# Plain pointwise products, products of the four-by-four convolution copied by pairs of banks, and the padded image as two tiles

## The chip, the cores and the metric

The kernel runs on one core of one Trainium2 chip. The metric is the device time of one execution in microseconds (us). TensorE is called PE in the profile, its weight loads PEld, VectorE DVE, ScalarE ACT, GpSimd POOL; SP issues most of the DMAs.

## The reference

Eight images of 512 channels and 32 x 32 points in fp32 go through two layers, each added to its input. Cut to what matters:

```python
# layer 0, on group-normed x: a bottleneck with attention, twice
t = cbs(x, cv1_w, ...)                 # 1x1 conv, norm, silu: 512 -> 512
ys = [t[:, :C], t[:, C:]]              # C = 256
for i in range(2):
    yi = ys[-1]
    z = cbs(yi, m_cv1_w[i], ..., pad=1)        # 3x3 conv, 256 -> 256
    z = bot_attention(z, ...)                  # qkv, 4 heads of 64, softmax over 1024
    ys.append(yi + silu(bn(conv1x1(z, m_cv2_w[i]))))
x = x + cbs(concatenate(ys), cv2_w, ...)       # 1x1 conv, 1024 -> 512
# layer 1, on group-normed x
h = prune(relu(bn(depthwise3x3(x))), 4.0)      # a channel whose maximum is below 4 becomes 0
h = prune(relu(bn(conv1x1(h, pw_w))), 1e-3)    # the pointwise convolution, 512 -> 512
x = x + h
```

## The kernel before

Images are done one after another, but an image's layer 1 is spread over the next image's layer 0. Every piece of work is a small function that is filed under a short name, and four strings, `FIRST`, `HEAD`, `TAIL` and `LAST`, say in which order the pieces are issued: image 0 runs `FIRST`, images 1 to 6 run `HEAD` and `TAIL`, image 7 `HEAD` and `LAST`. Each engine executes its own instructions in exactly that order (class `InOrder`), so a piece that has to wait holds back all that stands behind it on its engine. `p*3` means the next three pieces filed under `p`. All instructions recorded through these helpers show one line, L105, in the profile, so they are told apart by their tiles.

A three-by-three convolution (`conv3(l)`, l = 0 and 1) is done by a four-by-four transform. `dr` (DVE) combines rows of the padded image `yp[l]`, `d` combines columns into three operands that lie in `kr`, `vt` and `qy` (j = 0, 1, 2), `P` multiplies (PE), `Rc` copies the products out of PSUM (ACT), `R` and `B` (DVE) are the row and column sums of the way back, `E` ends them, and `Ez` (ACT) writes `z`. There are nine `P` for each convolution: for each j, part 0 makes four products of output half m = 0, part 1 two of each half, part 2 four of m = 1. Each `P` has 32 matmuls of 64 columns, pops one tile of 1 MB weights from the ring `wring` (five buffers, loaded from DRAM by SP) and asks for the next load. Before, the PSUM tile of two banks belongs to (j, m): half m of one j fills 768 of its 1024 columns, and it is copied in two steps (512 after the part of four, 256 after the part of two), 12 copies in a convolution. These tiles come from a pool of two, `big`, which the scores, the queries, keys and values also use.

After the convolution come `k`, `v`, `q` (products with `wqkv`, tiles `ps_qk` and `ps_v`), `ka`, `va`, `qa` (their copies by ACT), attention in 32 steps (`s` scores, `e` exponentials, `w` values, `p` sums on DVE, `n`, `nr`, `ns`, `sc` the normalization), then `m`, `ma`, `mr`: the 1x1 convolution `ps_m`, its activation, and the residual, which for l = 0 is written into `yp[1]`.

The pointwise convolution of layer 1 is done before, for images 0 to 6, by seven products in place of eight on quarters of the matrices (`by_quarters`, `one_pair`): `ot` makes four differences of the image `ht` on DVE (written into `pt`), `o` and `O` are two times seven products of two matmuls each, `ok` and `Ok` are copies by ACT, `ou` and `Ou` two times seven additions on DVE, and `oa`, `Oa` the closing activations. Its weights are combined during image 0 (`combine_more`) and kept in DRAM. The products write tiles of one bank, `acc`, of which there are three; attention's value sums, `ps_y` and `ps_m` use the same three. In `HEAD` the pieces `o` and `O` stand around the end of the first attention and in the second convolution. For image 7 the product is plain and in `LAST`.

`dp` loads the next image into `pt` (four DMAs on SP), `g` and the names behind it norm it. `t` are the eight depthwise taps per group of 128 channels on DVE (`ht<-xn,v_sb,ht`). `to_rows` adds the result of layer 0 to `xt` while it brings the points from an order by phase back into rows.

Of the kernel before, what the change touches and what calls it, by code (L numbers as in the profile page):

```python
# [15 lines left out]
P = 128  # L16
# [29 lines left out]
    g*4 gm gd g*2 gv gp gb ga*2 g*2 gm gd ta0 c gv gp fo gb ga*2 ta0 c ta0 ti0*2 fo ti0 ta2 c ca  # L46
    ti0*3 to0*2 ta2*2 c rl ca ti2*6 dr*3 to2*2 y ya dr*4 ta1*3 ti1*6 to1*2 rl dr*6 y ya y dr*3
    d*8 ya y ya d P Rc P*2 Rc*3 R*4 P*2 Rc R Rc R Rc B P Rc R*2 P Rc B P Rc*2 R*2 E B*2 Ez P Rc
    R*2 E Ez dw k*2 X ta0*2 k ka kp k ka kp ta0 ti0*2 v*2 va ti0*3 v ti0 v va ta1 q*3 qa ta1 q qa
    ta1 s e to0 ti1 s e p s e w to0 s p e w*2 s e p ti1*5 s e p*2 w s e to1 s e p w p w s e to1  # L50
    ta2 s e w*2 h p z s e p ta2*2 ti2*2 s e w s e w*2 ti2*4 s e w s to2*2 w*2 e s e p*2 rh s e w
    s e p*4 w h z s*2 w e*2 n s e w p s p*2 w*2 nr e nr*3 s e nc s e ns p w s e w*2 nc s e p*2 w
    h z s e s w s*2 p*2 e p e*2 p sc p w*2 sc w s e p w s e w p w*2 h z n nr*4 ns nc sc Q K m ma
    sc dp mr m*2 ma mr m ma dr mr ma mr dr*15 d*2 Q K nc d P*3 Rc*3 d*3 P*2 Rc R*2 d R*2 P Rc*3 d
    R d R Rc R*2 P Rc B*2 P Rc R*2 Rc P Rc B E Ez R*2 B E Ez dx cw X k*4 ka kp ka kp v*2 q v va v
    va cw*2 rk cw q qa q*2 qa s*2 e*2 p s e p w s e w s p cw*2 e s e w s e p rk p w s e p*2 s e w
    s e g*2 w*3 p h z s e w cw s e p*2 cw*2 rk s e w*2 s e w s p e rk s w p s w e p g*2 e p s w
    g*2 e s e w p h z p s w e g p w n nr s e nr p w g s e s p w nr e s e w s p w*2 nr p e s e w h
    ns p s e p nc*2 s e p w*2 s e p w s*2 e p w sc e p s e p w sc w*3 h z n nr*4 ns Q z Q sc*2
    nc*2 m*2 ma mr ma mr m ma m ma mr gm mr gd Q gv u A Q x i u A x i gp i*2 Q gb ga*4 Q im id Q  # L60
    iv A Q x ip i*2 ib b bm t*3 Q A t x i*2
# [3 lines left out]
    t c*2 t b bm im id ca c iv t dr*3 t*2 dr ip l dr*3 c t ca ib b lr dr*6 y dr*3 d*3 y*2 P Rc t  # L65
    d t ya R d*4 P*2 Rc*2 P R Rc R*2 Rc P Rc R*2 d t Rc ya P Rc P B P Rc*3 R*2 bm R ya B R B E P
    Rc R Ez R B b bm E Ez lp y ya k*4 ka kd ka X kd t*5 v t v va l v*2 va t lr t*2 q*2 t qa q*2
    qa s e t s e lp p t s w e s l s w e s p*2 w e*2 p w s e s p w t s w t e s p lr e*2 w*2 p h z
    s e w s t w s p*2 s e p e w*2 s e*2 w s t e p*3 s w s e w e t p*2 w lp t h z s*2 e w s e*2
    p*3 s e n w*2 s e s e w nr*3 s e nr t p*2 ns p l w*2 s e p lr lp w*2 h ot s e s w p ot s w*2  # L70
    s e p nc e p e w p s e ot s e w*2 p*2 z sc w*2 h z n nr nc o O ok Ok nr*3 ns o ou oa O*2 Ou
    sc*2 Oa m sc m*2 ma*2 m nc mr Ou ot mr ma mr dr ma o nc mr ou dr*3 O dr*5 o ou dr*7 d*3 Ou O
    o d*6 ou Ou*2 P*2 Rc*2 ou P R*2 Rc*2 R oa O P*3 o P Rc R*2 Rc*4 R B*2 R*2 Oa Ou B R P Rc*2 R
    ou oa B Oa dp P Rc o E Ez R*2 E Ez O k v*2 va X Ou ou oa k*2 ka kd k ka kd fr f fr f Oa fr*2
    f*2 dx v*2 va q*3 qa q qa s e s*2 e p e p w s e w s*2 e*2 p*3 w s*2 g e*2 w*4 s p e s e w p
    s*2 h g e g p z w s w p e*2 s*2 e w*2 g*2 s p e*2 g p*3 g s w*3 e p s e w h z s e s e p*2 w*2
    s p e p s n nr*3 w e p s nr g e p s w*4 e p s nc e s ns e nc w s h s p w*2 e p e s w s*2 e*2
    z sc p w p e p*2 w s sc e p w*3 h n nr*4 ns z
# [3 lines left out]
    Q*2 K r2 Q*2 sc*2 m K r0 m r2 m r1 nc*2 ma mr m ma*3 mr r0*2 mr r0 r1*2 Q gm Q*2 mr r1 u0 a0  # L82
    r2 u1 r2 gd Q u0*2 r3*2 gv r3 Q a1 x1 r3 gp gb ga x0 u0*2 a0 Q u0 x0 a0 i x0 i Q*2 i ga u0 ga
    a0 i im x0 Q id iv ip Q u1*2 ib u1 b u1 bm ga Q i Q t*2 u1 t a1*2 x1*2 u1 i a1 i x1 t i
# [3 lines left out]
    sc nc Q nc m ma m sc m*2 ma rg mr*2 ma*2 mr*2 Q*2 A x Q i*2 im id rg iv ip ib b bm t Q*2 t A  # L88
    x i*2 Q im t*2 Q id iv ip t ib t b t Q bm Q*2 t*2 A t l x i*2 im t lr lp id t iv ip ib t A b
    t*2 bm t Q o A x t l lr x i*2 lp o*3 im o t id t o*2 iv ip t o ib b bm o t*7 l lr lp t*5 l lr  # L90
    lp o*17 oa o oa fr f o oa o oa fr f o*3 oa*2 fr f oa*2 fr f
# [34 lines left out]
def fast_kernel(  # L126
# [54 lines left out]
    def load(dst, b):  # L181
# [14 lines left out]
    yp = [const_tile([P, 2, 4, 4, ROWS], f"yp{l}") for l in range(2)]  # L196
# [21 lines left out]
    ]  # L218

    PRODUCTS = ("a11", "a12", "s2", "s1", "s3", "a22", "s4")  # L220
    q_dram = [
        [dram.tile([P, 7, 2, P], F32, tag=f"q{i}_{p}", name=f"q{i}") for p in range(2)]
        for i in range(2)
# [28 lines left out]
    for t in yp:  # L252
        nc.gpsimd.memset(t, 0.0)
# [43 lines left out]
    def half_of(l, m, n):  # L297

        if l == 0:
            t = yp[0][:, m, :, 2 * n : 2 * n + 2, F // 4 :]  # L300
        else:
            t = yp[1][:, n].rearrange("p q (r k) x -> p q r k x", k=2)[:, :, :, m, F // 4 :]
        return t.rearrange("p q r x -> p r q x")
# [99 lines left out]
    def ring_sources():  # L403
        for b in range(B):
            for l in range(2):
                if b and l:
                    for p in range(2):
                        yield q_dram[1][p].rearrange("p q k o -> p (q k o)"), 1792
                for i in range(9):
                    yield u_dram[l][i].rearrange("p a b c d -> p (a b c d)"), 2048  # L410
                yield wqkv[:, l].rearrange("p k o -> p (k o)"), 1536
                if b == l == 0:
                    for m in range(2):
                        yield w2[:, :, m * P : (m + 1) * P], 1024
# [102 lines left out]
    plain = []  # L517

    def plain_pw():

        if not plain:
            plain.append(ring.pop(0).rearrange("p (k o) -> p k o", o=C))
        return plain[0]

    def by_quarters(rights, names, pairs):

        src, sums = rights
        b11, b12, b21, b22 = (
            (lambda i=i, n=n: src[:, 2 * i : 2 * i + 2, n * 512 : (n + 1) * 512])
            for i in range(2)
            for n in range(2)
        )
        t1, t2, t3, t4 = ((lambda t=t: t.rearrange("p (k n) -> p k n", k=2)) for t in sums)

        def less(o, x, y):
            nc.vector.tensor_tensor(o(), x(), y(), ALU.subtract)  # L540

        add(
            names[0],
            lambda: less(t1, b12, b11),
            lambda: less(t2, b22, t1),
            lambda: less(t3, b22, b12),
            lambda: less(t4, b21, t2),
        )
        right = dict(a11=b11, a12=b21, s2=t2, s1=t1, s3=t3, a22=t4, s4=b22)
        for kinds, finish in zip(names[1:], pairs):  # L550
            one_pair(right, kinds.split(), finish)

    def one_pair(right, kinds, finish):
        banks, kept, w = {}, [], []

        def product(name):
            if not w:
                w.append(ring.pop(0)[:, :1792].rearrange("p (q k o) -> p q k o", k=2, o=P))
            banks[name] = bank_tile("ps_q")
            for k in range(2):  # L560
                nc.tensor.matmul(
                    banks[name],
                    w[0][:, PRODUCTS.index(name), k, :],
                    right[name]()[:, k, :],
                    start=(k == 0),
                    stop=(k == 1),
                )
            if name == PRODUCTS[-1]:
                ring_load()

        def keep():
            t = work_tile("kept")
            kept.extend((t[:, :512], t[:, 512:]))
            nc.scalar.copy(kept[0], banks["a11"])

        def plus(o, x, name):
            nc.vector.tensor_tensor(banks[name] if o is None else kept[o], kept[x], banks[name], ALU.add)

        add(kinds[0], *[lambda name=name: product(name) for name in PRODUCTS])
        add(kinds[1], keep)  # L580
        add(
            kinds[2],
            lambda: plus(None, 0, "a12"),
            lambda: plus(0, 0, "s2"),
            lambda: plus(1, 0, "s1"),
            lambda: plus(0, 0, "s3"),
            lambda: plus(None, 1, "s3"),
            lambda: plus(None, 0, "a22"),
# [156 lines left out]
    def conv3(l):  # L745
# [17 lines left out]

        def by_rows(n, step):

            y = yp[l][:, n]
            if l == 0:
                o = [slots[:, slot[k], :, n] for k in range(6)]
                both = slots[:, :2, :, n]
# [1193 lines left out]
```

## Time and profile before

| | |
|---|---|
| median of 3 runs | 2728.95 us (2728.0 to 2729.35) |
| the profiled execution | 2721.36 us |
| its span, first to last instruction | 2719.6 us |
| mean granted TensorE clock | 0.986 |
| busy: PE, DVE, ACT, POOL | 2541.0, 2197.2, 1302.8, 133.2 us |
| one image to the next (second convolution to second convolution) | 327.7 to 328.6 us |
| in the image from 527.3 to 855.5 us: PE, DVE, ACT busy | 314.3, 269.1, 159.5 us |

A record of the profile is one hardware instruction; a full fp32 matmul of the program is two records. A row of a group has the engine, the operation, output and inputs, the shapes, the count, the busy time in us, the mean ns of one, then the idle time of the engine just before and what ended it. In a timeline the first column is the start, the second the length of the merged instructions, and a bracket holds the idle time before them and its releaser. Records of one engine may overlap, so the mean length of one matmul is longer than the distance between two.

### The profile page before, as it was taken

How to read it: one execution, taken by the hardware profiler on the slowest of the kernel's cores; microseconds unless marked ns; L12 is line 12 of the kernel's file. 1: busy time of each engine (PE TensorE's matmuls, PEld its weight loads, DVE VectorE, ACT ScalarE, POOL GpSimd, SP SyncE). 2: the span in 40 equal slices, each digit the busy share in tenths (PEclk: the TensorE clock that was granted, in tenths of full speed). 3: DMA queues.
4: the chain of work that ended last, by engine and by line, in shares of the span. 5: the costliest groups of instructions: out<-in, count | busy, mean ns of one | idle time of the engine just before them, and what ended most of it. 6: DMA issues, size and time to landing. Idle time of an engine off the chain costs nothing. (4 is left out here: it accounts for less than half of the span.)

```text
span 2719.6 us, 49469 instructions
## 1 busy us (share of the span) xinstructions
PE 2541.0 (93%) x20950; PEld 1242.5 (46%) x20950; DVE 2197.2 (81%) x3354; ACT 1302.8 (48%) x1748; POOL 133.2 (5%) x111
## 2 busy tenths in 40 slices
PE   4898999999999999989999899998999999999997
PEld 2535454443545445353453534535345453544433
DVE  7987778877988779887788877887788877988657
ACT  3453446354463544635356354554436444463534
POOL 1100001000010000000000000000000000010000
PEclk8999999999999999999999999999999999999999
DMA  8657223261413414153240621407024171322400
GB/s 286 222 177 266 87 107 106 78 221 45 157 49 126 169 59 159 29 197 102 70 161 19 225 75 62 164 16 283 17 82 143 32 268 32 124 87 92 154 16 33
DMA packets 97285, 325.97 MB, mean 120 GB/s; under 512 B 8224, under 2 KB 44832, under 8 KB 76704
## 3 DMA queue, kind: packets, MB, share of 16 engines
q1 hardware_dynamic: 89472, 304.64, 31.1%
q0 software_dynamic: 4032, 14.68, 3.0%
q10 hardware_dynamic: 3552, 3.41, 0.4%
q8 instruction: 166, 2.72, 0.4%
q14 instruction: 63, 0.52, 0.1%
HBM read 262.67 MB, written 43.25 MB: 112 GB/s over the span
## 5 line engine op out<-in xcount | busy, mean ns | idle before, releaser
L105 ACT ACTIVATE e<-ps_s 128x1024 f32<-128x1024 f32 x512 | 506.8, 1023 | 263.5 <-PE ps_s L105 214.0
L105 PE MATMUL ps_s<-qy,kr 64*64 64x512 f32 x4096 | 509.6, 592 | 8.1 <-ACT e L105 6.4
L105 PE MATMUL ps_av<-e,vt 64*64 64x512 f32 x4096 | 501.8, 590 | 0.0
L105 DVE TENSOR_TENSOR sum<-sum,e 128x1024 f32<-128x1024 f32 x384 | 470.2, 1224 | 37.3 <-ACT e L105 14.1
L105 DVE SCALAR_TENSOR_TENSOR ht<-xn,v_sb,ht 128x961 f32<-128x961 f32 (+1 forms) x256 | 317.9, 1247 | 8.6 <-ACT ht L105 5.0
L105 PEld LDWEIGHTS ps_s<-qy,kr 64*64 64x64 f32 x4096 | 160.1, 132 | 298.0 <-issue 186.6
L105 PEld LDWEIGHTS ps_av<-e,vt 64*64 64x64 f32 x4096 | 166.5, 133 | 276.2 <-issue 269.6
L105 PE MATMUL ps_qk<-z,wring 128*128 128x512 f32 x512 | 228.7, 595 | 11.6 <-ACT vt L105 7.7
L105 ACT COPY c<-ps_c 128x512 f32<-128x512 f32 x192 | 87.5, 482 | 303.5 <-PE ps_c L105 278.3
L105 DVE TENSOR_TENSOR sum<-e 128x1024 f32<-128x1024 f32 x64 | 78.0, 1219 | 127.6 <-ACT e L105 127.6
L105 PE MATMUL ps_c<-kr,wring 128*64 128x64 f32 x3072 | 116.4, 245 | 58.2 <-DVE kr L105 46.1
L105 PEld LDWEIGHTS ps_qk<-z,wring 128*128 128x128 f32 x512 | 95.7, 190 | 127.9 <-issue 104.3
L105 PEld LDWEIGHTS ps_c<-kr,wring 128*64 128x64 f32 x3072 | 110.9, 159 | 74.7 <-DVE kr L105 52.3
L105 PE MATMUL ps_y<-pt,w_sb 128*128 128x512 f32 x256 | 114.9, 602 | 11.2 <-ACT y L105 11.2
L105 PE MATMUL ps_c<-vt,wring 128*64 128x64 f32 x3072 | 102.3, 223 | 24.0 <-ACT c L105 8.9
L105 PE MATMUL ps_c<-qy,wring 128*64 128x64 f32 x3072 | 101.2, 223 | 23.1 <-ACT c L105 14.0
L105 DVE RECIPROCAL r<-ps_dn 128x128 f32<-128x128 f32 x128 | 109.5, 912 | 8.7 <-PE ps_dn L105 8.7
L105 PE MATMUL ps_cv<-pt,w_sb 128*128 128x512 f32 x256 | 116.0, 604 | 0.0
L105 PE MATMUL ps_v<-wring,z 128*128 128x256 f32 x512 | 114.6, 379 | 1.1 <-DVE kr L105 1.1
L105 PE MATMUL ps_m<-z,wm_sb 128*128 128x512 f32 x256 | 112.5, 592 | 0.0
L105 PEld LDWEIGHTS ps_c<-vt,wring 128*64 128x64 f32 x3072 | 95.0, 138 | 35.0 <-issue 13.6
L105 PEld LDWEIGHTS ps_c<-qy,wring 128*64 128x64 f32 x3072 | 94.8, 138 | 33.2 <-ACT c L105 17.4
(181 smaller groups left out, 3453.5 us busy)
## 6 DMA issues: line engine op xcount, KB each, us to landing
wring<-u SPq DMA_DIRECT2D x144, 1024.0 KB, 6.4
pt<-in_x SPq DMA_DIRECT2D x32, 512.0 KB, 7.3
rw<-r SPq DMA_DIRECT2D x64, 256.0 KB, 3.4
xt<-in_x SPq DMA_DIRECT2D x32, 512.0 KB, 6.2
out<-xt SPq DMA_DIRECT2D x32, 512.0 KB, 5.5
kr<-r POOLq DMA_DIRECT2D x28, 512.0 KB, 6.5
wring<-q SPq DMA_DIRECT2D x14, 896.0 KB, 7.0
u<-ucomp SPq DMA_DIRECT2D x48, 256.0 KB, 3.0
```

The source lines that it names most:

```text
L105: made = method(*args, **kwargs)
```

## The change

- The pointwise convolution of images 0 to 6 is multiplied plainly: eight pieces `o`, each four matmuls into one bank, and eight `oa`. `by_quarters`, `one_pair`, `combine_more` and their DRAM tiles are gone; the weights `wpw` come through the ring as one tile of 1 MB.
- A product of `conv3` writes one whole bank. Products 2n and 2n+1 share a tile of two banks, and one copy of 1024 columns empties it; the ninth has its own copy of 512. Five copies take the place of twelve.
- `yp[l]` is two tiles, one for each half of the channels (l = 0) or of the rows (l = 1).
- `to_rows` makes four additions over pairs of adjacent words in place of two over every fourth word.
- The four order strings are written anew.

```diff
-    yp = [const_tile([P, 2, 4, 4, ROWS], f"yp{l}") for l in range(2)]
+    yp = [[const_tile([P, 4, 4, ROWS], f"yp{l}_{n}") for n in range(2)] for l in range(2)]
...
                 if b and l:
-                    for p in range(2):
-                        yield q_dram[1][p].rearrange("p q k o -> p (q k o)"), 1792
+                    yield wpw.rearrange("p k o -> p (k o)"), 2048
...
-    def by_quarters(rights, names, pairs):
-    def one_pair(right, kinds, finish):
...
         if b < B - 1:
-            pairs = [lambda ps, low, n, p=p: close(2 * p + low, n, ps) for p in range(2)]
-
-            by_quarters((h_all, pt), ("ot", "o ok ou oa", "O Ok Ou Oa"), pairs)
+            def whole(m, n):
+                banks[m, n] = bank_tile("ps_pw")
+                part(m, n, range(KC))
+                if (m, n) == every[-1]:
+                    ring_load()
+
+            add("o", *[lambda e=e: whole(*e) for e in every])
+            add("oa", *[lambda m=m, n=n: close(m, n) for m, n in every])
...
         def products(j, part):
             u = ring.pop(0).rearrange("p (x i k o) -> p x i k o", x=4, i=2, k=2)
+            g = 3 * j + part
+            if g // 2 not in banks:
+                banks[g // 2] = big_tile("ps_c3")
+            ps = banks[g // 2][:, g % 2, :]
             for x in range(4):
-                m, row = UNITS[4 * part + x]
-                if (j, m) not in banks:
-                    banks[j, m] = big_tile("ps_c3")
-                ps = flat(banks[j, m])
+                row = UNITS[4 * part + x][1]
                 for i in range(2):
-                    at = place[row] * P + i * HD
+                    at = x * P + i * HD
...
-        def rows_copy(j, m, part):
-
-            if (j, m) not in copies:
-                copies[j, m] = work_tile("c1")
-            c = slice(0, 512) if part == 0 else slice(512, 768)
-            nc.scalar.copy(copies[j, m][:, c], flat(banks[j, m])[:, c])
+        def rows_copy(n):
+
+            t = copies[n] = work_tile("c1")
+            if n < 4:
+                nc.scalar.copy(t, flat(banks.pop(n)))
+            else:
+                nc.scalar.copy(t[:, :512], banks.pop(n)[:, 0, :])
...
-        for r in range(2):
-            nc.vector.tensor_tensor(o[..., r], i[..., r], o[..., r], ALU.add)
+        for q in range(4):
+            nc.vector.tensor_tensor(o[:, :, q], i[:, :, q], o[:, :, q], ALU.add)
...
-            combine_more(1, wpw)
```

Of the orders, the stretch of `HEAD` from the first `m` of the first attention to the second convolution's keys shows how they change:

```diff
-    sc*2 Oa m sc m*2 ma*2 m nc mr Ou ot mr ma mr dr ma o nc mr ou dr*3 O dr*5 o ou dr*7 d*3 Ou O
-    o d*6 ou Ou*2 P*2 Rc*2 ou P R*2 Rc*2 R oa O P*3 o P Rc R*2 Rc*4 R B*2 R*2 Oa Ou B R P Rc*2 R
-    ou oa B Oa dp P Rc o E Ez R*2 E Ez O k v*2 va X Ou ou oa k*2 ka kd k ka kd fr f fr f Oa fr*2
+    p z p sc w*2 h n nr*2 z nc nr*2 ns o*2 oa o oa sc*2 m sc m*2 ma*2 nc mr*2 dr*2 m dr*2 ma*2 mr
+    o oa dr*4 mr dr*6 o*2 oa dr*2 d*3 P*2 d nc d oa P d*4 P*2 Rc*2 P Rc R o P*3 o R*5 B*2 R oa R
+    B Rc B Rc R*2 E Ez R*2 E Ez k*4 fr f ka kd ka kd X q oa*2 q*3 dp qa*2 v fr f fr*2 f*2 dx v va
```

And the first convolution of `HEAD`, from its first `d` to the keys:

```diff
-    ... d*3 y*2 P Rc t d t ya R d*4 P*2 Rc*2 P R Rc R*2 Rc P Rc R*2 d t Rc ya P Rc P B P Rc*3 R*2
-    bm R ya B R B E P Rc R Ez R B b bm E Ez lp y ya k*4
+    ... d*2 y d y*2 t d t d*2 P*2 d P*2 Rc d R d ya Rc P*2 Rc P b P R*3 Rc R*2 ya R B R*2 B R B bm
+    E P Rc Ez R B R E Ez bm ya t*6 lp y k*3
```

## The prediction

> **What bounds the kernel now.** I read part 1 of the page first, then the table of waits of PE, then the timeline around one three-by-three convolution, then the groups kept apart by shape.
>
> ```profile
> PE 2541.0 (93%) x20950; PEld 1242.5 (46%) x20950; DVE 2197.2 (81%) x3354; ACT 1302.8 (48%) x1748; POOL 133.2 (5%) x111
> ```
>
> PE (TensorE) is busy 2541 of 2719.6 us and DVE (VectorE) 2197: PE bounds the kernel on the whole, and DVE where PE stands still. What PE waits for:
>
> ```profile
> PE ps_c L105 <- DVE kr L105: 46.1, 28, 12.0
> PE ps_c L105 <- ACT c L105: 28.4, 48, 0.7
> PE pm L105 <- DVE mv L105: 20.3, 10, 8.6
> PE ps_c L105 <- DMA wring<-u: 8.8, 15, 1.7
> PE ps_qk L105 <- ACT vt L105: 7.7, 7, 1.1
> ```
>
> Columns are total us, times, longest. 48 waits are three in each of 16 convolutions. Where one lies, in the second convolution (l = 1) of an image, during which the pointwise products (`ps_q`) of the image before are fillers:
>
> ```profile
> 507.50 7.03 PE L105 MATMUL ps_m<-z,wm_sb 128*128 128x512 f32 x16
> ...
> 510.23 0.69 DVE L105 TENSOR_TENSOR yp<-m,yp 128x512 f32<-128x512 f32 x1 [1.69 <-ACT m L105]
> ...
> 514.37 8.99 PE L105 MATMUL ps_q<-pt,wring 128*128 128x512 f32 x20
> ...
> 527.30 0.70 PE L105 MATMUL ps_c<-kr,wring 128*64 128x64 f32 x8 [3.95 <-DVE kr L105]
> ...
> 549.59 2.09 PE L105 MATMUL ps_c<-qy,wring 128*64 128x64 f32 x64 [0.73 <-ACT c L105]
> ...
> 557.70 1.88 PE L105 MATMUL ps_qk<-z,wring 128*128 128x512 f32 x4
> ...
> 564.13 5.42 PE L105 MATMUL ps_qk<-z,wring 128*128 128x512 f32 x12 [1.10 <-ACT vt L105]
> ```
>
> PE has nothing to do for 3.95 us before the first product and stands again before others. One full matmul is two records; 16 of them go from 507.50 to 514.37, 0.43 us a record. The wait of 3.95 recurs in every later image, and 507.50 to 557.70 (50.2 us) is 50.0 to 50.6 in the six others. In the first convolution (l = 0) DVE is the limit:
>
> ```profile
> 709.00:720.00 11.00, 10.86 (x26) 4.53 (x24) 10.90 (x19) 5.00 (x8) 1.34 (x1) 1.00 0.00 1
> 720.00:760.00 40.00, 35.32 (x628) 27.44 (x629) 38.95 (x77) 22.93 (x41) 3.71 (x3) 1.00 0.73 245
> ```
>
> After the length the columns are PE, PEld, DVE, ACT, POOL, clock: DVE is busy 38.95 of 40.
>
> **The skill.** *PSUM — Partial Sum Buffer* (The four PSUM rules) puts one matmul's output in one bank of 512 fp32. A tile of this convolution is two banks, and part 0 and part 1 of a product write different ones, yet the trace has the wait `ps_c <- ACT c` in front of the second: the wait is kept for the tile, not the bank. *SBUF — State Buffer* (Door 1) says that lines are 16 bytes and at least two hits on one are needed for full speed. The trace agrees: an addition in `to_rows` over every fourth word takes 637 ns, one of 256 packed elements 417. *DMA: Bandwidth & Descriptors* (Bandwidth) gives 436 GB/s as the ceiling; one fortieth of the window 527 to 557 us reached 448.
>
> **The change, part by part.** Prices:
>
> ```profile
> L105 PE MATMUL ps_q<-ht,wring 128*128 128x512 f32 x168 | 75.8, 601 | 0.0
> L105 DVE TENSOR_TENSOR xt<-c,xt 128x256 f32<-128x256 f32 x100 | 58.3, 637 | 2.3 <-ACT c L105 2.1
> L105 ACT COPY c<-ps_c 128x512 f32<-128x512 f32 x96 | 56.5, 588 | 212.7 <-PE ps_c L105 188.3 <-issue 22.2 <-DVE mid L105 2.2
> L105 DVE TENSOR_TENSOR ps_q<-kept,ps_q 128x512 f32<-128x512 f32 x56 | 37.4, 690 | 19.1 <-issue 10.2 <-PE ps_q L105 9.0
> L105 ACT COPY c<-ps_c 128x256 f32<-128x256 f32 x96 | 36.0, 375 | 90.8 <-PE ps_c L105 90.0 <-DVE c L105 0.6
> L105 ACT COPY qy<-ps_qk 128x1024 f32<-128x1024 f32 x32 | 32.4, 1012 | 67.8 <-PE ps_qk L105 67.8
> L105 DVE TENSOR_TENSOR pt<-ht 128x1024 f32<-128x1024 f32 x14 | 17.0, 1216 | 0.0
> ```
>
> *Plain pointwise product.* 28 matmuls an image become 32: 8 more records, 3.43 us, 24.0 us in seven images, on the path. DVE loses 4 subtractions (4 x 1.22) and 14 additions (14 x 0.69): 14.4 us an image. Off the path they are worth nothing; the 12.4 us inside the l = 1 stage are counted below only through it. ACT loses two copies (0.58 each), hidden. Two weight loads of 896 KB become one of 1 MB, so of the five ring buffers one, not two, is held through l = 1. The first image loses 8 DVE additions (4.6 us) and 15 DMAs of its preparation under attention, where PE is full: 0.
>
> *Whole banks by pairs.* Twelve copies (6 x 0.588 + 6 x 0.375 = 5.8 us) become four of 1024 (1.012) and one of 512: 4.6 us. No product now writes a tile with a copy of it pending; tile n waits only for the copy of n-2, which is 3.8 us of products earlier against 1.2 (0.2 to start, 1.0 to run). The 28.4 us go. What is late next is DVE: its row sums start only after two products and the longer copy.
>
> *Two tiles.* `dr` of half 0 need not stand behind the writes of half 1. Two memsets on POOL become four halves, before anything waits: 0.
>
> *The l = 1 stage, first `ps_m` to first `ps_qk`.* A product is 1.89 us (two of l = 0 go from 723.55 to 727.33). PE before: 6.9 + 36 records of `ps_q` 15.5 + 9 x 1.89 = 39.4 of 50.2, so 10.8 stand still. PE after: `ps_m` 6.9, three pointwise banks 10.3 (product 0 can start at 17.2), six products 11.3, a bank 3.4, three products 5.7, a bank 3.4: 41.0. DVE after: first `mr` at 2.7 (510.23 - 507.50), four `mr` 2.75, sixteen `dr` 8.0, the first `d` 1.76 and `kr` 0.95: 16.2, ahead of 17.2, so **the 3.95 goes**. Then, from product 0: the other seven `d` to 6.9; row sums of 1.8 each, the third waiting for the third pair's copy (12.5), so four end at 16.1; both `B` 5.1: 21.2; the fourth copy is there at 19.8; a row sum 1.8 and `E` 0.7: 23.7; z by ACT 1.24: 25.0. So `ps_qk` begins at 17.2 + 25.0 = 42.2. I add 1.0 for weights: a 1 MB load at 415 GB/s is 2.5 us against 1.89, and four lie ready. 43.2 against 50.2: **-7.0**. Five banks fall in this stage, three before it (24 records for 20): **+1.7**. The `vt` wait: with keys multiplied in one run before values, its cover is ready: **-1.1**.
>
> *The l = 0 stage.* DVE sets it; one depthwise tap (1.25 us) moves out of it, some row sums move: **-1.0** (0 to -1.5). PE's four us of waits there are not gained.
>
> *`to_rows`.* 2 additions of 637 ns become 4 of 128 elements, 50 times. Output pairs now share a line, but the input hops between two rows. From below 0.28 us each (DVE operations of 128 packed elements take 285 ns), from above 0.39 (417 for 256 and 285 for 128 leave 150 fixed, and 637 then has 1.9 ns an element): -0.15 to +0.3 a call, -1.2 to +2.4 us an image on DVE, in a stage where DVE is busy 51.9 of 69 us. I take 0.
>
> *Moved pieces.* The four loads of the next `pt` go behind the query products on SP, some 12 us later; they take 7.4 to land and are read after the values' products and several attention steps. The POOL adds of positions keep their place behind the keys' copies. First image: DVE carries it, -2. Last: taps on DVE feed the weights, 0 (3 either way).
>
> **Sum.** -7.0 + 1.7 - 1.1 - 1.0 = -7.4 an image, seven times -51.8, -2: -53.8. The profiled execution took 2721.36 us (span 2719.6), so 2667.6; the median of the runs stands 7.6 above that execution: **2675**.
>
> **Rivals.** *Weights bound the products.* For: 15 waits for `wring` already, and products come faster. If loads stay at the 287 GB/s of that window, each takes 3.65: the fifth lands 8.4 after product 0, the ninth 23.0 instead of being wanted at 18.6, and the stage is about 46: +2.8 x 7, 2695. Against: that rate includes gaps in which nothing was asked for.
>
> *The first product's inputs stay late.* If `kr` comes no earlier against PE, only some 1.9 of copy waits and 1.1 of `vt` are gained against 3.43: +0.4 an image, 2730. Against: 3.3 us of subtraction and additions stood between `mr` and `kr`.
>
> *Pair copies in series with DVE* (slower). If every row sum arrives before its copy, each of five tiles shows the copy and its start, 1.2 us, on DVE's chain: 6 us a convolution, 15 of them, +90: 2765. It decides from where DVE is ahead: by my count it comes at 6.9 to a copy ready at 5.0, level at the second, 1.9 early at the third only. The two last copies also need a free work buffer out of eleven, which a DVE row sum frees.
>
> **How the numbers follow.** The main case 0.63 (2655 to 2692), weights 0.14, no gain 0.07, serial copies 0.13, more gain than summed 0.03. The range 2650 to 2724 leaves out the last two mostly and part of the third. About 0.2% (5.5 us) is what a measurement can tell: faster 0.79, same 0.07, slower 0.14.
>
> **What would show it.** Right: `ps_c <- ACT c` nearly gone, `ps_c <- DVE kr` down from 46 to under 22 (the first image's 12.0 stays), `ps_qk <- ACT vt` gone, about 21,006 matmul records, the l = 1 stage 42 to 44 us. New waits of a `ps_qk` for z of about 1 us in l = 1 and up to 5 in l = 0 belong to it. Wrong: `ps_c <- wring` above 20 us (weights), a wait for `kr` of 3 us or more in each image, or DVE waiting for `ACT c` by 40 us or more.

## The result, and the profile after

The changed kernel takes 2685.9 us in the median of three runs (2683.96 to 2689.96), the kernel before 2728.95 (2728.0 to 2729.35). The ratio is 0.9846, interval 0.9823 to 0.9868. Four later runs of the changed kernel gave 2691.21 (2685.89 to 2700.12) and a ratio of 0.9869 (0.9849 to 0.9888). Those four are the base of the experiments, called **the base** below. The forecast was 2675, range 2650 to 2724. Profile against profile it is 2721.36 to 2689.96: -31.4, where the sum said -53.8. So the direction and the range held. Of the forecast gain 11 us are missing by the medians of three runs, 22 profile against profile, and 19 in the later runs beside the kernel before of the same time.

Busy times, from part 1 of the page after (share of the span, then instructions). PE has the 21,006 matmul records that were forecast, and DVE is 96 us lighter:

```profile
PE 2547.8 (95%) x21006; PEld 1247.9 (46%) x21006; DVE 2101.3 (78%) x3320; ACT 1278.3 (48%) x1622; POOL 129.9 (5%) x113
```

What PE waits for, from the table of waits after (total us, times, longest):

```profile
PE ps_c L103 <- issue: 49.7, 32, 5.7
PE ps_c L103 <- DVE kr L103: 26.7, 16, 22.2
PE ps_qk L103 <- ACT z L103: 16.6, 15, 3.9
PE pm L103 <- DVE mv L103: 13.3, 10, 8.0
```

The 48 waits for ACT's copies (28.4 us) and the waits for `vt` (7.7) are gone. Of the waits for `kr`, 22.2 are now the first image's (12.0 before, and 11.2 more then for `y` in front of the last `ps_y`), and the other fifteen are 0.3 us each. New at the top stands `issue`, time in which PE waited for nothing that the profile can name. In the table of before it stood third:

```profile
PE ps_c L105 <- issue: 21.5, 23, 6.5
```

The second convolution of image 2, from PE's timeline after (start, length, then in brackets the idle time before and its releaser):

```profile
835.61 7.03 PE L103 MATMUL ps_m<-z,wm_sb 128*128 128x512 f32 x16
842.48 10.46 PE L103 MATMUL ps_pw<-ht,wring 128*128 128x512 f32 x24
852.87 0.45 PE L103 MATMUL ps_c<-kr,wring 128*64 128x64 f32 x8
853.73 5.58 PE L103 MATMUL ps_c<-kr,wring 128*64 128x64 f32 x184 [0.41 <-DVE kr L103]
...
863.80 1.03 PE L103 MATMUL ps_c<-vt,wring 128*64 128x64 f32 x26 [0.76 <-DMA wring<-u]
865.58 1.32 PE L103 MATMUL ps_c<-vt,wring 128*64 128x64 f32 x38 [0.75 <-issue]
```

From 835.61 to 852.87 it is 17.26 us, and the prediction said 17.2. PE no longer stands 3.95 us ahead of the products. It stands inside them instead.

Two prices, from the groups after, kept apart by shape (busy us, mean ns):

```profile
L103 ACT COPY c<-ps_c 128x1024 f32<-128x1024 f32 x64 | 64.8, 1013 | 303.3 <-PE ps_c L103 303.3
L103 DVE TENSOR_TENSOR xt<-c,xt 128x128 f32<-128x128 f32 x200 | 43.5, 286 | 3.1 <-ACT c L103 2.9
```

The pair copy is what was used (1.012). Of the two bounds for `to_rows`, 0.28 and 0.39 us, the lower is right: four times 286 ns is 1.14 us a call against 1.27. It is the time of packed elements, though the input still hops between two rows.

**Where the waits for `issue` come from.** The first convolution of image 7, PE's timeline after:

```profile
2335.79 2.91 PE L103 MATMUL ps_c<-vt,wring 128*64 128x64 f32 x94
2341.15 1.63 PE L103 MATMUL ps_c<-vt,wring 128*64 128x64 f32 x44 [2.45 <-issue]
2342.56 4.09 PE L103 MATMUL ps_c<-qy,wring 128*64 128x64 f32 x83
2347.09 3.37 PE L103 MATMUL ps_c<-qy,wring 128*64 128x64 f32 x109 [0.45 <-issue]
```

The trace's list of DMA packets has two queues of kind "instruction" (packets, MB, share of 16 engines' time, in the whole run):

```profile
q8 instruction: 167, 2.74, 0.4%
q14 instruction: 62, 0.51, 0.1%
```

The packets of q8 are 16 KB each, and 2.74 MB is what PE's 21,006 matmuls and 21,006 weight loads need at 64 bytes an instruction (2.69 MB). In this stretch two of them run from 2338.75 to 2339.68 and from 2344.78 to 2345.74, so PE goes on 1.47 and 1.35 us after their ends. The gaps of more than 0.4 us for `issue` inside the products all end 1.1 to 1.7 us after a q8 packet, in every trace of this study, but for one of 5 to 6.5 us in image 0. Within a convolution of l = 0 they lie 127 or 128 matmul records apart. So 128 matmuls with their 128 weight loads use up one packet, which is 64 bytes an instruction again. That much was read from the traces alone; what makes a packet late was left to the experiments.

### The profile page after: what moved, and what is told of

Read it like the earlier page. It is cut to its first block, busy times and chain, and to the rows that moved or that the text cites. A ratio compares the mean times of both kernels' runs of the same rounds, so it can differ in the third digit from the quotient of the medians.

```text
span 2688.2 us, 49311 instructions
## 1 busy us (share of the span) xinstructions
PE 2547.8 (95%) x21006; PEld 1247.9 (46%) x21006; DVE 2101.3 (78%) x3320; ACT 1278.3 (48%) x1622; POOL 129.9 (5%) x113
## 3 DMA queue, kind: packets, MB, share of 16 engines
q8 instruction: 167, 2.74, 0.4%
## 5 line engine op out<-in xcount | busy, mean ns | idle before, releaser
L103 ACT ACTIVATE e<-ps_s 128x1024 f32<-128x1024 f32 x512 | 506.4, 1024 | 272.8 <-PE ps_s L103 257.7
L103 DVE SCALAR_TENSOR_TENSOR ht<-xn,v_sb,ht 128x961 f32<-128x961 f32 (+1 forms) x256 | 323.5, 1269 | 9.2 <-ACT ht L103 5.0
L103 PE MATMUL ps_pw<-ht,wring 128*128 128x512 f32 x512 | 232.4, 608 | 2.3 <-DVE wring L103 2.3
L103 ACT COPY c<-ps_c 128x1024 f32<-128x1024 f32 (+1 forms) x80 | 74.3, 929 | 314.0 <-PE ps_c L103 313.0
L103 PEld LDWEIGHTS ps_pw<-ht,wring 128*128 128x128 f32 x512 | 96.9, 193 | 123.6 <-issue 119.1
L103 PE MATMUL ps_c<-kr,wring 128*64 128x64 f32 x3072 | 101.6, 229 | 33.2 <-DVE kr L103 26.7
L103 PEld LDWEIGHTS ps_c<-kr,wring 128*64 128x64 f32 x3072 | 97.3, 144 | 48.0 <-DVE kr L103 35.2
L103 DVE RECIPROCAL r<-ps_dn 128x128 f32<-128x128 f32 x128 | 109.5, 913 | 11.2 <-PE ps_dn L103 11.2
```

What stands on the lines that cost most here:

```text
L103: made = method(*args, **kwargs)
```

## The experiments

All are edits of the changed kernel unless said otherwise. "Stage l = 1" is first `ps_m` to first `ps_qk`, "stage l = 0" first product to first `ps_qk`, as means over images 1 to 7; in the base 44.9 and 27.8 us.

**The base.** The changed kernel again.

> The changed kernel again, as the base of the runs beside it. Both theories: 2684 to 2690 us; waits of ps_c for issue about 49 us in some 30 places, each ending 1.2 to 1.6 us after the end of a 16 KB packet of the instruction queue.

Measured: 2691.21 us, just above what was expected, with `issue` 49.5 us in 33 places. Medians of this kernel on two occasions differ by 5 us, so smaller differences of the whole time are not read below. The traced execution of the base is its longest, 2700.12 us; the two mean stages of images 1 to 7 differ from those of the first trace of this kernel by 0.2 us at most.

**Longer matmuls between the products.**

```diff
-        add("y", *[lambda m=m, n=n: half(m, n) for m in range(2) for n in range(2)])
+        halves = (range(2), range(2, KC))
+        add("y", *[lambda m=m, n=n, ks=ks: half(m, n, ks) for m in range(2) for n in range(2) for ks in halves])
...
-    oa P d*4 P*2 Rc*2 P Rc R o P*3 o R*5
+    oa P d*4 P o P Rc*2 P Rc R o P*2 o P o R*5
...
```

In the first convolution two halves of `ps_y` are moved in between the products in the same way, from in front of the keys.

> The banks of ps_y and of ps_pw are multiplied in halves of two input chunks, and some of these halves are put between the products of the convolution. Theory 1 (PE runs out of fetched instructions in a long run of 64-column products, since 128 products with their weight loads are 16 KB of instructions and use them up in 3.95 us): longer matmuls between them give the fetch time, so the waits of ps_c for issue fall from 49 to between 25 and 38 us and the time by 6 to 14 us, to 2672 to 2680. Theory 2 (the waits called issue are a late copy or row sum in another form): the halves move no copy and no row sum earlier, so the waits stay at 45 to 52 us and the time within 3 us of the changed kernel's.

Measured: 2702.69 us, +11. The waits for `issue` did fall, to 23.0 us, as theory 1 had it, and no time was gained. From the table of waits of this kernel:

```profile
PE ps_qk L103 <- ACT z L103: 48.0, 16, 5.6
PE ps_c L103 <- issue: 23.0, 19, 5.7
```

The idle time moved from in front of the products to in front of the keys (19.2 us there in the base), where the moved matmuls no longer fill it. A product behind a longer matmul is as late as one behind a gap, and DVE's row sums start from it: DVE waits for the pair copies for 55.5 us here and 54.1 in the base. Both stages keep their lengths (28.1 and 44.8 us). So the expectation fell, and the reading that fits is that an `issue` wait costs through the lateness of the products. The 11 us lie mostly between the first keys of l = 0 and the first `ps_m` behind them, 91.3 us an image in place of the 90.0 and 90.3 of the two traces of the changed kernel; why was not tested.

**The waits for copies put back.**

```diff
+            if g in (0, 6) or (l == 0 and g == 2):
+                nc.scalar.copy(ps, ps)
             ring_load()
```

> Behind products 0 and 6 of each convolution, and behind product 2 where l = 0, ACT copies the bank just written onto itself; the next product writes the other bank of that tile, so the wait for a copy that the change took away is back, 40 times of 48. Nothing else is changed. By the prediction's step (28.4 us of such waits go, 0.59 each) the time rises by 24 us or more, to 2710 or more. Theory 1 (instruction fetch): where l = 0 each such wait is time in which the fetch catches up, so the waits for issue fall from 49 to about 30 us or less while the waits for ACT rise to 25 to 35, and the time rises by only 5 to 15 us, to 2691 to 2701.

Measured: 2705.37 us, +14.2, within what theory 1 gave and well under the 24. From its table of waits:

```profile
PE ps_c L103 <- issue: 34.3, 25, 5.7
PE ps_c L103 <- ACT ps_c L103: 28.3, 40, 1.0
```

40 waits are back, 28.3 us in all. In stage l = 0 they took the place of waits for `issue` (29.4 to 13.9 us) and the stage kept its length (28.1); in stage l = 1 `issue` stayed (19.5 and 19.6) and the stage grew by 1.3. By this run about half of what the pairs took away was time that PE would have spent on `issue` anyway. The added copies are also work of ACT, whose part in the 14 us this run doesn't separate.

**No weight loads beside the products.**

```diff
-                for i in range(9):
+                for i in range(9 if b == 0 else 0):
                     yield u_dram[l][i].rearrange("p a b c d -> p (a b c d)"), 2048
...
-            u = ring.pop(0).rearrange("p (x i k o) -> p x i k o", x=4, i=2, k=2)
+            u = ring.pop(0) if first else w1_sb.rearrange("p k o -> p (k o)")
...
-            ring_load()
+            if first:
+                ring_load()
```

> Images 1 to 7 multiply by the weights of the first pointwise convolution, which stay in SBUF, in place of the transformed weights of the three-by-three convolutions, which are not loaded for them: 126 loads of 1 MB are left out. Theory 1a (PE's instruction fetch has a pace of its own): the waits of ps_c for issue stay at 40 to 55 us, the waits for wring (2.7) go, and the time falls by 2 to 8 us. Theory 1b (the instruction packets are held up by the weight loads on the same 16 DMA engines): the waits for issue fall under 20 us, and the time by 20 to 35 us, to 2651 to 2666.

Measured: 2654.34 us, -36.9: theory 1b. PE's waits for `issue` in this kernel:

```profile
PE ps_c L103 <- issue: 12.7, 5, 5.7
```

The same convolution as above, PE's timeline in this kernel:

```profile
2303.78 5.59 PE L103 MATMUL ps_c<-kr,w_sb 128*64 128x64 f32 x184 [0.32 <-DVE kr L103]
2309.19 5.87 PE L103 MATMUL ps_c<-vt,w_sb 128*64 128x64 f32 x192
2314.89 5.77 PE L103 MATMUL ps_c<-qy,w_sb 128*64 128x64 f32 x192
2320.59 3.70 PE L103 MATMUL ps_y<-pt,w_sb 128*128 128x512 f32 x8
2327.45 3.48 PE L103 MATMUL ps_qk<-z,wring 128*128 128x512 f32 x5 [3.16 <-ACT z L103]
```

Nine products without a gap, 17.66 us in each of the seven images where the base takes 21.8 to 23.3. All gaps of over 0.4 us for `issue` that are left belong to image 0, which still loads. Where no gap interrupts them, PE's records follow each other at 29.2 ns in both kernels (the median over stretches of 32), so the loads don't slow the multiplying itself. The DMA view of 2303 to 2321 us in this kernel, and then of 2336 to 2354 in the changed one (packets, MB, share of 16 engines' time):

```profile
q8 instruction: 4, 0.07, 1.6%
```

```profile
q1 hardware_dynamic: 926, 6.52, 95.3%
q8 instruction: 3, 0.05, 1.0%
```

With nothing beside them the q8 packets start at 2307.10, 2310.88, 2314.65 and 2318.35, 3.75 us apart. In the changed kernel they stand in a crowd that takes 95.3% of the DMA engines' time, and start some 6 us apart. The packet itself takes 0.92 to 0.96 us there and 0.95 to 1.24 us without the loads: it starts late, it does not run long.

**Half the bytes.**

```diff
-    yield u_dram[l][i].rearrange("p a b c d -> p (a b c d)"), 2048
+    yield u_dram[l][i].rearrange("p a b c d -> p (a b c d)")[:, : 2048 if b == 0 else 1024], ...
...
-    u[:, x, i, k, o : o + HD],
+    (u if x < 2 or image[0] == 0 else own)[:, x, i, k, o : o + HD],
```

> Of each load of convolution weights in images 1 to 7 the first half alone is loaded (0.5 MB of 1 MB), and the other half of each product multiplies by the weights of the first pointwise convolution. As many loads, as many semaphores, as many instructions, half the bytes. Theory (bytes in the DMA engines hold up the instruction packets): waits of ps_c for issue fall from 49 to under 20 us and the time to 2652 to 2668. Rival (the loads' issue and their semaphores hold PE, not their bytes): the waits stay over 35 us and the time over 2680.

Measured: 2672.63 us, -18.6, half of what no loads at all gave; `issue` 41.2 us. Neither of the theory's numbers was met; of the rival's two the waits were, the time was not. Without image 0, whose loads are whole in all of these, the gaps of over 0.4 us for `issue` sum to 35.3 us in the base, 26.6 here and 0 without loads. So the delay grows with the bytes. In the last six products of l = 0 the DMA engines are busy for 98% of the time in the base and for 79% here, and packets are still late. The number of loads is not excluded as a part of it.

**Fewer loads in the second half.**

```diff
-            ring_load()
+            if g <= 4:
+                ring_load()
...
-        todo["q"].append(lambda last=todo["q"].pop(): (last(), ring_load()))
+        todo["q"].append(lambda last=todo["q"].pop(): (last(), ring_load(5)))
```

> The loads that the last four products of each convolution release, which fetch weights for later work (four of the thirteen that fall into a convolution), are issued after the query products in place of beside the convolution. Nothing else is changed and nothing is left out. Theory (an instruction packet stands behind the weight loads that fill the DMA engines): the second half of a convolution's products has fewer loads beside it, so the waits of ps_c for issue fall from 49 to between 20 and 38 us and the time by 6 to 20 us, to 2671 to 2685. Rival 1 (the loads of the first half make the delay, or the four are too late for the next use): waits stay over 42 us or turn into waits for wring, and the time is at 2688 or above. Rival 2 (five loads in one go hold up the next image's input): no gain, with new waits of pm in front of the next stage.

Measured: 2690.96 us, no difference; `issue` 46.1 us, `wring` 4.9. Those are the numbers of rival 1, but the trace shows that the edit did not do what it was meant to where the waits are. SP has an order of its own and doesn't wait for PE's query products: in l = 0 it issued the loads as soon as buffers of the ring came free. In the first convolution of image 2 the nine loads start 2.6, 4.4, 6.3, 8.3, 11.3, 13.2, 17.8, 20.9 and 22.7 us after the first product (2.6, 4.4, 6.3, 8.3, 12.0, 13.8, 17.6, 19.5 and 22.2 in the base), and in the last three products of l = 0 the DMA engines are busy for 98% of the time in both. Only in l = 1 did loads move, from some 19 to 27 us to 30 us and later, but in the last three products there the base has 0.5 us of gaps for `issue` in images 1 to 7 together, beside 13.0 in l = 0. So whether later loads would free the packets of l = 0 is not tested.

**Loads cut in four.**

```diff
-            nc.sync.dma_start(o, src[0])
...
+            for i in range(parts):
...
+                nc.sync.dma_start(o[:, i * n : i * n + n], src[0][:, i * n : i * n + n])
```

> Each load of 1 MB or 768 KB into the weight ring is issued as four or three DMAs of 512 columns (256 KB each) in place of one. The bytes, the ring, the products and their order are those of the changed kernel. In its trace an instruction packet that is due while all 16 DMA engines are busy starts 1 to 3.5 us late, after 0.5 to 1.4 MB of load packets, which is about one load; with loads of half the size it was 0.1 to 0.6 MB. Theory (a packet waits for one whole DMA on its engine, some 2.5 us for 1 MB): with DMAs of 256 KB it waits some 0.6 us, the waits of ps_c for issue fall from 49 to 20 us or less (the first image keeps 6 to 14), and the time by 12 to 28 us, to 2663 to 2679. Rival (it waits for its share among all the load packets outstanding, however they are cut): the waits stay over 40 us and the time within 5 us of 2691, or above it if smaller DMAs move fewer bytes a second, with waits for wring over 10 us.

Measured: 2694.95 us (ratio to before 0.9883, 0.9865 to 0.99, beside 0.9869 of the base); `issue` 47.4 us. The rival: cutting the loads brings nothing, so it isn't the length of one DMA that keeps a packet waiting.

**Half the instructions.**

```diff
-                        for o in (0, HD):
-                            nc.tensor.matmul(ps[o : o + HD, at : at + HD], u[:, x, i, k, o : o + HD], ...)
+                        nc.tensor.matmul(ps[:, at : at + HD], u[:, x, i, k, :], ...)
```

> The products of the convolution use all 128 weight columns in one matmul, in place of two matmuls of 64 columns: half the instructions for the same output, with the same weight loads. Theory (the packets of instructions stand behind weight loads that fill the DMA engines; e_noload without the loads has 12.7 us of issue waits and 2654 us): half the packets are wanted, so the waits of ps_c for issue fall from 49 to under 20 us. The pace of a product is the open part: 1.96 us now without stalls; 32 records at the rate of the ps_m records (0.43 us for 512 columns of moving data, so 0.054 for 64) would be 1.7. Then 2654 to 2676 us. Rival (the stage's end is DVE's row sums whatever PE does, as e_mix suggests, which lost its issue waits and no time): the waits move to ps_qk for z, and the time stays within 6 us of 2691.

Measured: 2906.61 us, +215. The waits for `issue` are gone but for the one in image 0, and q8 has 131 packets in place of 167. The pace is what was mis-estimated. From the groups of this kernel:

```profile
L103 PE MATMUL ps_c<-vt,wring 128*128 128x64 f32 x1536 | 193.7, 293 | 0.0
```

Nine products of l = 0 take 32.59 us in images 1 to 7, in place of 17.66 without stalls: a product of 32 full-width records 3.6 us, one of 64 half-width records 1.96. The Trainium skill, *TensorEngine Tiling (Array Packing)* (Theoretical Speedup), gives up to two times for a small dimension of 64; here it is 1.85. The many small instructions are the price of that.

**DVE's additions put back.**

```diff
-    ... mr*2 dr*2 m dr*2 ma*2 mr o oa dr*4 mr dr*6 o*2 oa dr*2 d*3
+    ... mr*2 xx dr*2 m xx dr*2 ma*2 mr o oa xx dr*4 mr xx dr*6 o*2 oa xx dr*2 d*3
...
```

> In images 1 to 7 DVE makes five additions of 128x512 more (0.69 us each, 3.45 in all, results not used) among the pieces between the first residual and the transformed columns of l = 1, in the place of some of the 14 additions that the change took out. By the prediction DVE is ready 1.0 us ahead of PE there (16.2 and 17.2): so 2.4 us an image are seen as a wait of the first product for kr of some 2.8 us, and the time is +15 to +20 us on 2691. If DVE sets the end of the whole stage in any case, +3.45 an image, +24 us. If the row sums and the fetch of instructions have slack of their own, the wait for kr comes and the stage's end moves by less than 1 us an image.

Measured: 2713.67 us, +22.5, near the 24 of the second case, though the wait for `kr` is the 2.7 us of the first. The first product comes at 20.0 in place of 17.26 in images 1 to 7, and the stage grows by 3.4: nearly all of the 3.45 reaches its end. So DVE sets the beginning of the products. That its row sums set the end as well is not shown: between the first product and the keys DVE itself waits for the pair copies for 3.5 us a stage (2.9 in the base).

**Four pointwise matmuls fewer.**

```diff
-                part(m, n, range(KC))
+                part(m, n, range(KC), every.index((m, n)) in (1, 3, 6, 7))
...
```

Where the last argument is true, `part` leaves out k = 3.

> Of the 32 matmuls of the pointwise product the last input chunk of four banks is left out in images 0 to 6: 28 are left, as many as the kernel before has. The prediction priced the four at 3.43 us an image, all on the path: -24 us, so 2665 to 2669 on a base of 2691. If those inside the convolution's stage lie beside DVE work that sets its end (two of the four), only half is gained: 2676 to 2682.

Measured: 2687.2 us, -4.0, which is no difference that can be told (ratio 0.984, 0.9816 to 0.9864, which overlaps the base's), where the price was -24. Of the four, the one ahead of `ps_m` gives its 0.86 us an image. The one between `ps_m` and product 0 gives nothing: product 0 stays at 17.25 and waits for `kr` instead (32.2 us in all, 26.6 in the base). The two behind give 0.4 together, little more than the 0.2 by which two traces of one kernel differ. Stage l = 0, which the edit doesn't touch, grew by 0.9. One reading is that fewer instructions ahead move the place at which a packet runs out; it was not tested.

**One padded image.**

```diff
-    yp = [[const_tile([P, 4, 4, ROWS], f"yp{l}_{n}") for n in range(2)] for l in range(2)]
+    yp_all = [const_tile([P, 2, 4, 4, ROWS], f"yp{l}") for l in range(2)]
+    yp = [[t[:, n] for n in range(2)] for t in yp_all]
```

> The padded image is one tile with two halves again, in the order of pieces of the changed kernel. The prediction gave this edit no price. What it can bring back is a wait of ACT, which writes the second half of yp of l = 0, for the row differences that DVE takes from the first: an image's first product of l = 0 would come later by 0 to 1 us. Expected: 0 to +7 us on 2691, most likely no difference that can be measured.

Measured: 2690.76 us, no difference. The two tiles do nothing by themselves in this order.

**The kernel before, without weight loads.** The edit of the fourth experiment in the kernel before.

> The kernel before, with the same left out as in e_noload: images 1 to 7 multiply by the first pointwise weights in place of the convolutions' weights, which are not loaded. If the prediction's steps are right but for the fetch of instructions, the change is worth 50 to 58 us between this kernel and e_noload (2654), so 2704 to 2712 us. If the change is worth its measured 36 to 43 us whatever is loaded, 2690 to 2697 us. If the weight loads held the kernel before as much as the changed one, under 2697 too, with its issue waits of 20 us gone.

Measured: 2707.76 us. Beside it the changed kernel without loads is 2654.34: the change is worth 53.4 us there by the medians, which come from two chips, and 50.6 between the two profiled executions. The prediction's sum was 53.8.

## Why the prediction was right, and where its sum was not

Stages in us, means over images 1 to 7 of the traces of the result; the last column is the difference of the two kernels without loads:

| | before | after | difference | forecast | without loads |
|---|---|---|---|---|---|
| stage l = 1 | 50.3 | 44.7 | -5.6 | -7.0 | -6.3 (48.5 to 42.2) |
| stage l = 0 | 26.4 | 27.8 | **+1.4** | -1.0 | -1.1 (25.5 to 24.5) |
| pitch of images 1 to 7 | 328.2 | 321.9 | -6.3 | -7.4 | -8.7 (325.9 to 317.2) |

*Stage l = 1.* The list of PE's and DVE's work was right to the first product: 17.26 for 17.2. Its end was worked out as 42.2 without weights and is 42.2 without loads. The term that was mis-sized is the 1.0 added for weights: the stage is 44.7, so it is 2.5. It was also put down to the wrong thing. The waits for `wring` are 2.7 us in the whole run, so the weights are there in time; their transfers keep the instructions away. So the stage ends above the 42 to 44 that the prediction named as a sign.

*Stage l = 0.* This is the step that failed. DVE was taken to set the end, and "PE's four us of waits there are not gained". Without loads that is right to 0.1. With them the copy waits gone from PE are replaced by waits for instructions, the products end no earlier (22.9 us after the first one begins in the kernel before, 22.8 in the changed one), the copies and row sums follow them, and the stage is 1.4 longer. No part of the sum had a term for PE's instructions. The waits that the prediction lists leave out the third of the table before, the 21.5 us for `issue`.

*DVE's lead at the first product* was forecast as 1.0 us. The two experiments on it bound it: with 0.86 us less work on PE the product came no earlier, and 3.45 more on DVE moved it by 2.75. So PE and DVE are level there, with at most 0.7 to spare.

*Plain pointwise product.* The three banks ahead of `ps_m` are 24 records for 20, 1.72 us in the trace, as forecast. That all eight records, 24.0 us in seven images, lie on the path is too much: with four matmuls left out, the one outside the stage gave its time and the other three at most half a matmul's together.

*The rest of an image.* The wait for `vt` is gone, and from keys to first scores it is 22.1 to 20.7 (-1.4 for -1.1). Not foreseen, from the new order: the last denominators (`ps_dn`) at the end of the first attention take 2.0 in place of 3.2 us (image 3), and the waits for the norm's `mv` fall from 20.3 to 13.3 in all.

*First image.* -2 was about right to the first product, 68.96 to 66.14 us. The sign "`kr` under 22" still failed, with 26.7, by the 22.2 of this image. Then both convolutions of image 0, the first of image 1 and the stretches ahead of it and behind it went the other way by 1.1 to 2.4 us each, and `ps_m` of image 1 starts at 514.6 in place of 507.5.

*The rivals.* "Weights bound the products", +2.8 an image, was right about the resource and wrong about the way: no wait for `wring` over 20 us was seen, and the test that the prediction named for it was blind to the fetch. "Pair copies in series with DVE" seemed to have come: in the base DVE's row sums wait for copies for 54.1 us, where the mark was 40.

```profile
DVE c L103 <- ACT c L103: 27.5, 14, 4.0
DVE mid L103 <- ACT c L103: 26.6, 14, 3.4
```

Without loads they are 15.0 in all, so the copies were late because the products were. "The first product's inputs stay late" did not happen.

*In all.* The loads cost the kernel before 19.8 us (2727.57, its median beside that run, to 2707.76) and the changed one 36.9 (2691.21 to 2654.34): that takes some 17 us of the gain. Without loads the gain is 51 to 53 us, near the sum, but that the totals agree so closely is in part luck. There the first `ps_m` of image 1 comes 6.0 us later (508.9 to 514.9) where the sum had it earlier, and each later image gains 8.7 us for 7.4, through the parts that were not foreseen. The two misses largely cancel. That 2685.9 lies in the 2655 to 2692 of the main case is no proof of it either: some 17 us that it had no term for are in the result.

## What to carry to other kernels

Wait time taken away is only worth what its next limit leaves, and the next limit can be one that the waits had covered: count PE's instructions as traffic too, and ask what they queue behind where many small matmuls run beside full-rate loads. Time that the profile calls `issue`, in the same place in stage after stage, is worth a look at the instruction queue's packets. To find what a shared resource costs, run both kernels without the load on it: here that gave the mechanism, and told the terms of the sum that it had spoilt from those that were wrong by themselves. And look in the trace whether an edit moved what it was meant to move: a DMA that is issued later in the program can start at the same time as before.

## What the hardware showed that was not expected

PE's instructions come in packets of 16 KB, 256 instructions, and PE goes on 1.1 to 1.7 us after a packet's end when it had run dry. Without stalls 128 of these matmuls and their weight loads, one packet's worth, take 3.74 us at 29.2 ns a matmul. With idle DMA engines the next one is there in time; with busy ones it starts late, by 2.3 us in the mean of 41 packets of the base, against the record of PE at which the same packet starts without loads. Loading half of the bytes gave half of the time; cutting the same bytes into smaller DMAs gave none. How the engines choose between an instruction packet and the loads outstanding stays open.
